# The first weights by one-partition rows and eighths, and the router's products beside the first maxima, in an attention and expert kernel

## The chip, the cores and the metric

The kernel runs on one core of a Trainium2 chip. The metric is device time in microseconds (us) of one execution; lower is better. TensorE multiplies matrices, VectorE (DVE), ScalarE (ACT) and GpSimd (POOL) work on vectors, and SyncE (SP) issues most of the transfers between memory and the core. Every engine works through its own list of instructions in order and waits where an instruction needs another engine or a transfer.

## The reference

Four sequences of 512 tokens with 256 numbers each go through two residual blocks. In the first, each sequence has its own expert, chosen by the largest of eight numbers in `cond_8`; its three matrices make a gated layer, and 16 heads of attention with one shared key and value follow. In the second, the weights of a linear layer are mixed from eight matrices by the same numbers, and a router sends each token to two of eight experts with a capacity of 128 rows per group.

```python
expert = jnp.argmax(opcode_onehot, axis=-1)
hidden = jax.nn.silu(up) * gate           # up, gate: x with the expert's two matrices
out = jnp.einsum('bsh,bdh->bsd', hidden, wd) + bd[:, None, :]
...
w_bot = jnp.einsum('bg,got->bot', y, weight * mask[None, :, :])
x2 = jnp.einsum('bnt,bot->bno', x, w_bot) + bias
...
logits = jnp.einsum('gth,he->gte', xg, w_router)
...
x = x + attn(cond(x, cond_8))
x = x + ffn(cond2(x, cond_8))
```

All of it is in float32.

## The kernel before

The program is one long list written out by hand; the order in the text is the order on each engine. It has four stages.

**The start.** SP loads `cond_8`, broadcast to 128 partitions (`cond_sb`, L86), and the transposed x of sequence 0. VectorE works out `rows` (L114 to L122): for each sequence the row at which its expert's weights begin, with the partition's own number added (`rowp`), so that an indirect transfer can use it too. SP reads the row of partition 0 into a register (L159) and `load_cond` issues the weights of the sequence: the up and gate matrices in quarters (`w`, 256 KB each, L162) and, behind the first quarter, the down matrix with the three biases (`wd`, 517 KB, L164). Sequences 0, 1 and 2 are loaded so; those of sequence 3 by two indirect transfers of POOL (`fetch_cond`, L147). Until weights are there TensorE multiplies a tile of zeros, seven times (L94). [...]

**The gated layer.** `hidden(b, hc)` (L280) computes one of four blocks of 128 hidden units: two products for up into the only bank of tag "a" (L291), two for gate into a bank of tag "x" (L293), Silu on ScalarE with its bias from `wd` (L295), the product on VectorE (L296). `down(b, dc)` (L275) follows. VectorE mixes the weights of the second block in between (`mixed`, L262 and L264, into `wb_sb`), four operations at a time.

**Attention.** A unit of work is a step; a sequence has 16, the kernel 64. Step n has two parts on TensorE: `maxima` of the step six ahead (four products in 32-row tiles, L387, each read by one VectorE reduction, L391) and `exponentials` of its own (four such products, L416, each read by one ScalarE operation, L420). `weigh` (L434, 32-column tiles) multiplies the exponentials of the step before with the values. Before step 0 lies the lead: six `maxima`, each with a piece of the gated layer of sequence 3 or 2 behind it (`before_steps`, L808). `beside` (L734) lists what else is put into each of a sequence's steps: entries (1, ...) work for the next sequence (queries, keys, values `v`), (-1, ...) and (-2, ...) for those before (output projection, `rT`, `mix`, router, scatter of rows). `behind` (L772) adds four calls to sequence 0: at steps 5 and 9 `turn_mixed` (L700: four transposes of `wb_sb`, a copy by ScalarE) of two sequences, at steps 7 and 11 `route_mixed` (L711: the product of these with the router's matrix, so that the router's logits come out of the same product as the layer itself; for sequence 0 also that of the bias).

A step whose side work has TensorE products is `dense`: its order is maxima, exponentials, side work, maxima, exponentials, both halves of `weigh`. Any other step puts half of `weigh` between the two halves. The names that make a step dense are in `ON_PE` (L770).

**The experts.** The rows are gathered in tiles of up to 256, with two products and a weighted scatter-add each. The change doesn't touch this stage.

PSUM has eight banks: three of tag "m", one "a", four "x" (`BANKS`, L72).

Of the kernel before, what the change touches and what calls it, by code (L numbers as in the profile page):

```python
# [10 lines left out]
F32 = mybir.dt.float32  # L11
I32 = mybir.dt.int32
AF = mybir.ActivationFunctionType
ALU = mybir.AluOpType
AX = mybir.AxisListType
PSUM = bass.MemoryType.PSUM

P = 128
B = 4
# [3 lines left out]
NE = 8  # L23
# [14 lines left out]
WROW = 1024 + 10  # L38
# [3 lines left out]
def adaln_attn_ffn_kernel(  # L42
# [22 lines left out]
    nc = tc.nc  # L65
    mm = nc.tensor.matmul

    const = ctx.enter_context(tc.tile_pool(name="const", bufs=1))
# [6 lines left out]
    def bank(tag):  # L75
# [6 lines left out]

    od = tc.dram_tile([B, 4, P, T], F32, name="od")

    cond_sb = const.tile([P, B, NE], F32, name="cond_sb")
    nc.sync.dma_start(  # L86
        cond_sb.rearrange("p b e -> p (b e)"), cond[0:1, :].to_broadcast([P, B * NE])
    )


    nil = const.tile([P, 512], F32, name="nil")
    nc.vector.memset(nil, 0.0)
    for _ in range(7):
        mm(bank("x"), nil[:, 0:P], nil, start=True, stop=True)  # L94
    nc.scalar.activation(const.tile([P, 1], F32, name="nil1"), nil[:, 0:1], AF.Silu)

# [1 line left out]
    rev = const.tile([P, NE], F32, name="rev")  # L98
    nc.gpsimd.iota(
        rev, pattern=[[-1, NE]], base=NE, channel_multiplier=0,  # L100
        allow_small_or_imprecise_dtypes=True,
    )

    rowp = const.tile([P, 1], F32, name="rowp")
    nc.gpsimd.iota(
        rowp, pattern=[[0, 1]], base=NE * P, channel_multiplier=1,
        allow_small_or_imprecise_dtypes=True,
    )


    rows = const.tile([P, B], I32, name="rows")
    top = const.tile([P, B], F32, name="top")
    first = const.tile([P, B, NE], F32, name="first")
    nc.vector.tensor_reduce(top, cond_sb, AX.X, ALU.max)  # L114
    nc.vector.tensor_tensor(
        first, cond_sb, top.unsqueeze(2).to_broadcast([P, B, NE]), ALU.is_equal
    )
    nc.vector.tensor_tensor(
        first, first, rev.unsqueeze(1).to_broadcast([P, B, NE]), ALU.mult
    )  # L120
    nc.vector.tensor_reduce(top, first, AX.X, ALU.max)
    nc.vector.tensor_scalar(rows, top, -float(P), rowp, ALU.mult, ALU.add)  # L122

    attn_ctx = ctx.enter_context(ExitStack())
    apool = attn_ctx.enter_context(tc.tile_pool(name="apool", bufs=1))
# [11 lines left out]
    def cond_tiles():  # L137
        w = wexp.tile([P, 2, F], F32, name="wi_sb").rearrange("p c f -> p (c f)")
        w2 = wexp.tile([P, F // P, D], F32, name="wo2_sb").rearrange("p c f -> p (c f)")
        w_of.append((w, w2))  # L140
        return w, w2

    def fetch_cond(b):

        w, w2 = cond_tiles()
        for t, src in ((w, wcond), (w2[:, 0:WROW], wcond2)):
            nc.gpsimd.indirect_dma_start(  # L147
                out=t,
                out_offset=None,
                in_=src,  # L150
                in_offset=bass.IndirectOffsetOnAxis(ap=rows[:, b : b + 1], axis=0),
            )

    def load_x(b):
        nc.sync.dma_start(xT_sb[:, :, ts(b, T)], xT[:, :, ts(b, T)])

    def load_cond(b):

        row = nc.sync.value_load(rows[0:1, b : b + 1], min_val=0, max_val=(NE - 1) * P)  # L159
        w, wd = cond_tiles()  # L160
        for hc in range(4):
            nc.sync.dma_start(w[:, ts(hc, 512)], wcond[ds(row, P), ts(hc, 512)])  # L162
            if hc == 0:
                nc.sync.dma_start(wd[:, 0:WROW], wcond2[ds(row, P), :])  # L164


    load_x(0)
    load_cond(0)
    load_x(1)
    load_cond(1)  # L170
    nc.sync.dma_start(m2_sb, mask2.rearrange("p c o -> p (c o)"))
# [6 lines left out]
    def load(ap, shape, name):  # L178
# [22 lines left out]
        out=upto, in_=ones, compare_op=ALU.is_ge, fill=0.0, base=0,  # L201
        pattern=[[1, P]], channel_multiplier=-1,
    )
    def numbers(name, shape, pattern, base, step):
# [20 lines left out]
        out=through, in_=ones[:, 0 : NE * NE].rearrange("p (a e) -> p a e", a=NE),  # L225
        compare_op=ALU.is_ge, fill=0.0, base=0, pattern=[[1, NE], [-1, NE]],
        channel_multiplier=0,
# [35 lines left out]
        else:  # L263
            nc.vector.scalar_tensor_tensor(wb, w, c, wb, ALU.mult, ALU.add)  # L264

    fetch_cond(3)
    mixing = [(b, g) for b in range(B) for g in range(NE)]
    hid_of = {}

# [441 lines left out]
    def route_mixed(b):  # L711
# [23 lines left out]
        [(1, "q0"), (-2, "rank0")],  # L735
        [(1, "q1"), (-2, "rank1")],
        [(-1, "values"), (1, "k"), (-2, "places"), (-2, "rows")],
        [(1, "v"), (-2, "send")],
        [(-1, "inv"), (-2, "row0")],
        [(-2, "row1")],  # L740
        [(-1, "norm0"), (-1, "norm1"), (-2, "row2")],
        [(-1, "out0"), (-1, "out1"), (-2, "row3")],
        [(-1, "out2"), (-1, "out3")],
        [(-1, "rT0"), (-1, "rT1")],
        [(-1, "mix0"), (-1, "mix1")],
        [(-1, "mix2"), (-1, "mix3")],
        [],
# [21 lines left out]
    ]  # L769
    ON_PE = ("q", "k", "v", "out", "rT", "mix")  # L770

    behind = {  # L772
        5 + 2 * b + 2 * n: (f, b) for b in range(0, B, 2)
        for n, f in enumerate((turn_mixed, route_mixed))
    }

    final = {
        0: ["inv0"], 2: ["values1"], 4: ["inv1", "norm0", "norm1"],
        6: ["out0", "out1", "out2", "out3"], 7: ["rT0", "rT1"],
# [7 lines left out]
    def side(b, k):  # L787

        for off, name in (last if b == B - 1 else beside)[k]:
            to = b + off  # L790
            if not 0 <= to < B:
                continue
            if name[:5] == "pairs":
                first_pairs(name[5:])
                continue
            if off == 1:
                if name == "q0":
                    projection[to] = project(to)
                projection[to][name]()
            else:  # L800
                work[to][name]()
        if b == 0 and k in behind:
            f, to = behind[k]
            f(to)
            f(to + 1)


    before_steps = [  # L808
        [(hidden, B - 1, 0), (down, B - 2, 0)],
        [(down, B - 2, 1), (hidden, B - 1, 1)],  # L810
        [(hidden, B - 1, 2)],
        [(hidden, B - 1, 3)],
        [(down, B - 1, 0)],
        [(down, B - 1, 1)],
    ]
    for m in range(LEAD):
        maxima(m, (0, 1, 2, 3))
        if m == 3:
            shifted(0)
        for f, b, k in before_steps[m]:  # L820
            f(b, k)
        while mixing:
            mixed(*mixing.pop(0))
    c1.close()
# [237 lines left out]
    for n in range(STEPS + 1):  # L1062
        m = n + LEAD
        if n in (0, 26, 42, 56):
            residual((0, 26, 42, 56).index(n))
        b, k = divmod(n, 16)
        names = [name for _, name in (last if b == B - 1 else beside)[k]] if b < B else []
        dense = (b == 0 and k in behind) or any(
            name.rstrip("0123") in ON_PE and (b > 0 or name in projection[0]) for name in names
        )  # L1070
        if m >= STEPS:
            if n < STEPS:
                exponentials(n, (0, 1, 2, 3))
            if n == STEPS:

                up(0, 0)
            weigh(n - 1, (2, 3))
            weigh(n - 1, (0, 1))
            if n < STEPS:
                side(b, k)  # L1080
        elif dense:

            maxima(m, (0, 1))
            exponentials(n, (2, 3))
            side(b, k)
            maxima(m, (2, 3))
            exponentials(n, (0, 1))
            if n > 0:
                weigh(n - 1, (2, 3))
                weigh(n - 1, (0, 1))  # L1090
        else:

            maxima(m, (0, 1))
            exponentials(n, (2, 3))
            if n > 0:
                weigh(n - 1, (2, 3))
            maxima(m, (2, 3))
            exponentials(n, (0, 1))
            side(b, k)
            if n > 0:  # L1100
                weigh(n - 1, (0, 1))
        if m < STEPS and m % 4 == 3:
            shifted(m // 4)
# [153 lines left out]
```

## Time and profile before

| | us |
|---|---|
| median of three runs (lowest, highest) | 665.79 (663.47, 666.86) |
| the profiled execution's own time | 666.94 |
| its span | 665.1 |
| TensorE busy | 645.8 (97%) |
| VectorE busy | 323.8 (49%) |
| ScalarE busy | 225.8 (34%) |
| POOL busy | 112.8 (17%) |
| start to first real product | 10.09 |
| lead (six maxima) | 70.8 to 105.9 |
| 64 steps begin | 105.85 |

The span is the time between the first and the last instruction in one profiled execution; its own time has the launch around it. In the profile a float32 product counts as two passes, so "x4" of L291 are two products. A busy TensorE is one whose passes follow each other, whatever they compute. The share of the clock granted was 0.99: half speed from about 371 to 375 us, at the start until about 6, and full elsewhere.

### The profile page before, as it was taken

The page shows a single profiled execution, that of the slowest core. Times are in us where ns is not written, and L with a number is a line of the kernel's source. Part 1 is how long each engine was busy: PE and PEld are TensorE (multiplying, and loading weights), DVE is VectorE, ACT ScalarE, POOL GpSimd, SP SyncE. Part 2 cuts the span into 40 slices and gives each one's busy share as a digit, 9 for nine tenths or more (in the row PEclk, how much of TensorE's full clock was granted, in tenths as well). Part 3 has the DMA queues.
Part 4 walks back from the last instruction along what each step waited for, and adds up shares of the span by engine and source line. Part 5 has one row for each costly group of instructions (what it writes and reads, how often), then busy time and mean ns, then how long its engine had stood idle before and what let it go on. Part 6 is the DMA issues. An engine that isn't in the chain of part 4 may idle for free.

```text
span 665.1 us, 10593 instructions
## 1 busy us (share of the span) xinstructions
PE 645.8 (97%) x3994; PEld 394.3 (59%) x3994; DVE 323.8 (49%) x782; ACT 225.8 (34%) x400; POOL 112.8 (17%) x149
## 2 busy tenths in 40 slices
PE   9999999999999999999999899999999999999991
PEld 3444433444334434343344378888999999988881
DVE  1164854666667677867976625372222222221210
ACT  1122114665664565546545541322011111121110
POOL 1600000000000000400040412235321222222231
PEclk9999999999999999999999899999999999999996
DMA  6942982200132114320134399329799999974411
GB/s 217 384 137 65 300 270 81 62 17 17 43 106 94 35 31 133 132 65 18 50 132 138 107 389 283 111 97 310 230 288 314 326 333 316 353 232 115 89 19 24
DMA packets 65147, 107.47 MB, mean 162 GB/s; under 512 B 6848, under 2 KB 26944, under 8 KB 64960
## 3 DMA queue, kind: packets, MB, share of 16 engines
q1 hardware_dynamic: 49200, 86.38, 38.8%
q0 software_dynamic: 7008, 10.63, 7.9%
q10 hardware_dynamic: 8880, 9.71, 4.6%
q8 instruction: 33, 0.54, 0.3%
q14 instruction: 26, 0.21, 0.1%
HBM read 79.59 MB, written 26.98 MB: 160 GB/s over the span
## 4 chain that ended last, share of the span: by engine, by line
PE 95%; DVE 1%; DMA 1%; issue 1%; POOL 0%; SPq 0%; POOLq 0%; DVEq 0%
PE ps_m L387 20%; PE ps_m L996 19%; PE ps_x L1026 18%; PE ps_a L434 10%; PE ps_a L291 4%; PE ps_x L275 4%; PE ps_x L293 4%; PE ps_x L514 2%; PE ps_x L546 2%; PE ps_x L325 2%; PE ps_x L416 2%; PE ps_x L94 1%; PE ps_x L340 1%; PE ps_a L981 1%; PE ps_x L535 1%
## 5 line engine op out<-in xcount | busy, mean ns | idle before, releaser
L391 DVE TENSOR_REDUCE negm<-ps_m 128x1 f32<-128x512 f32 x250 | 160.6, 685 | 64.8 <-PE ps_x L416 52.1
L420 ACT ACTIVATE e<-ps_x 128x512 f32<-128x512 f32 x244 | 132.5, 594 | 112.9 <-PE ps_x L416 100.3
L387 PE MATMUL ps_m<-k,q 32*128 32x512 f32 x500 | 151.7, 639 | 0.4 <-DVE negm L391 0.4
L416 PE MATMUL ps_x<-q,k 32*128 32x512 f32 x488 | 141.5, 643 | 1.4 <-DMA q<-nmT 1.4
L996 PE MATMUL ps_m<-xT,wi_sb 128*128 128x128 f32 (+1 forms) x800 | 130.3, 321 | 0.0
L1026 PE MATMUL ps_x<-wo_sb,e 128*128 128x256 f32 x576 | 128.5, 379 | 0.0
L996 PEld LDWEIGHTS ps_m<-xT,wi_sb 128*128 128x128 f32 x800 | 118.9, 191 | 10.1 <-issue 0.4
L1026 PEld LDWEIGHTS ps_x<-wo_sb,e 128*128 128x128 f32 x576 | 107.6, 190 | 13.8 <-issue 0.2
L1000 ACT ACTIVATE e<-ps_m 128x512 f32<-128x512 f32 x72 | 42.8, 597 | 193.8 <-PE ps_m L996 158.3
L387 PEld LDWEIGHTS ps_m<-k,q 32*128 32x128 f32 x500 | 45.7, 183 | 56.6 <-issue 24.4
L1037 POOL DMA_INDIRECT out_dram<-y,to_row x36 | 56.0, 1557 | 127.9 <-DVE y L1036 36.2
L434 PE MATMUL ps_a<-e,v 128*32 128x256 f32 x1024 | 75.6, 391 | 0.5 <-issue 0.3
L434 PEld LDWEIGHTS ps_a<-e,v 128*32 128x32 f32 x1024 | 24.0, 109 | 77.7 <-issue 64.3
L983 DVE COPY xT<-ps_a 128x256 f32<-128x256 f32 (+1 forms) x23 | 12.2, 529 | 99.5 <-PE ps_a L981 94.0
L1036 DVE TENSOR_SCALAR y<-ps_x,w 128x256 f32<-128x256 f32 x36 | 17.4, 483 | 77.2 <-PE ps_x L1026 77.2
L667 POOL DMA_INDIRECT xp<-x,to_i x32 | 32.0, 1000 | 57.7 <-DVE negm L391 28.5
L416 PEld LDWEIGHTS ps_x<-q,k 32*128 32x128 f32 x488 | 39.1, 183 | 4.5 <-issue 4.3
L596 POOL TENSOR_SCALAR x<-mk 128x4 f32<-128x4 f32 x4 | 0.8, 209 | 209.3 <-DVE mk L593 209.3
L296 DVE SCALAR_TENSOR_TENSOR hid<-ps_x,wo_sb,sg 128x512 f32<-128x512 f32 x16 | 12.0, 749 | 46.2 <-PE ps_x L293 46.2
L291 PE MATMUL ps_a<-xT_sb,wi_sb 128*128 128x512 f32 x64 | 30.5, 598 | 0.0
L293 PE MATMUL ps_x<-xT_sb,wi_sb 128*128 128x512 f32 x64 | 30.1, 592 | 0.0
L1034 POOL CAST to_row<-at 128x1 int32<-128x1 f32 x36 | 19.0, 527 | 58.5 <-DVE at L1019 58.5
(153 smaller groups left out, 444.1 us busy)
## 6 DMA issues: line engine op xcount, KB each, us to landing
wi_sb<-in_wi_dram SPq DMA_DIRECT2D x25, 1024.0 KB
wo_sb<-in_wo_dram SPq DMA_DIRECT2D x25, 1024.0 KB
xp<-zeros ACTq DMA_DIRECT2D x1, 8712.0 KB
q<-qd SPq DMA_DIRECT2D x8, 512.0 KB
od<-stage SPq DMA_DIRECT2D x15, 256.0 KB
wi_sb<-in_wcond_dram SPq DMA_DIRECT2D x12, 256.0 KB
xt<-xp SPq DMA_DIRECT2D x11, 264.0 KB
xT_sb<-in_xT_dram SPq DMA_DIRECT2D x4, 512.0 KB
```

The source lines that it names most:

```text
L291: mm(pu, wu[:, c, :], xT_sb[:, c, ts(b, T)], start=c == 0, stop=c == 1)
L293: mm(pg, wg[:, c, :], xT_sb[:, c, ts(b, T)], start=c == 0, stop=c == 1)
L387: mm(pm, q[32 * j : 32 * j + 32, i, ts(hg, P)], k[32 * j : 32 * j + 32, :], start=True, stop=True,)
L391: nc.vector.tensor_reduce(nm[:, i, j : j + 1], pm, AX.X, ALU.max, negate=True)
L416: mm(px, k[rows_j, ts(sc, P)], seqs[u // 4]["q"][rows_j, :, ts(u % 4, P)], start=True, stop=True,)
L420: nc.scalar.activation(e_of[n][:, :, j, :].rearrange("p h (i t) -> p i h t", i=4), px.rearrange("p (i h t) -> p i h t", i=4, h=4), AF.Exp,)
L434: i = mm(pa_of[u][32 * hh : 32 * hh + 32, j0 * P : (j0 + nj) * P], seqs[b]["v"][:, sc, :], e[:, hh, j0 : j0 + nj].rearrange("p j n -> p (j ...
L667: i = nc.gpsimd.indirect_dma_start(out=xp, out_offset=bass.IndirectOffsetOnAxis(ap=s["to_i"][:, k, ch : ch + 1], axis=0), in_=s["x3"][:, c ...
L996: mm(ph[:, ts(k, n)], wi_of[u][:, c, ts(f0 + k, P)], xT_of[u][:, c, :], start=c == 0, stop=c == 1,)
L1000: nc.scalar.activation(hT_of[u][:, f0 : f0 + each].rearrange("p f t -> p (f t)"), ph, AF.Gelu_apprx_tanh,)
L1026: mm(po[:, 0:D], hT_of[u][:, fc, ts(h, P)], wo_of[u][:, fc, :], start=fc == 0, stop=fc == F // P - 1,)
L1037: i = nc.gpsimd.indirect_dma_start(out=out_rows, out_offset=bass.IndirectOffsetOnAxis(ap=to, axis=0), in_=y, in_offset=None, compute_op=AL ...
```

## The change

`cond_8` is loaded to one partition (`cond1`) and the rows are worked out there, without the partition's number; the broadcast `cond_sb`, which `mixed` needs, is loaded behind the first sequence's weights. Sequence 0's first quarter of up and gate becomes two transfers of 256 columns, the first for up, the second for gate. Sequence 3's weights are loaded by `load_cond` like the others. Four products on zeros are left of seven. `turn_mixed` and `route_mixed` move from steps 5 to 11 of sequence 0 into the lead, and the next sequence's values `v` from step 3 to step 9.

```diff
-    cond_sb = const.tile([P, B, NE], F32, name="cond_sb")
-    nc.sync.dma_start(
-        cond_sb.rearrange("p b e -> p (b e)"), cond[0:1, :].to_broadcast([P, B * NE])
-    )
+    cond1 = const.tile([1, B, NE], F32, name="cond1")
+    nc.sync.dma_start(cond1.rearrange("p b e -> p (b e)"), cond)
...
-    for _ in range(7):
+    for _ in range(4):
         mm(bank("x"), nil[:, 0:P], nil, start=True, stop=True)
...
-    nc.vector.tensor_scalar(rows, top, -float(P), rowp, ALU.mult, ALU.add)
+    nc.vector.tensor_scalar(rows, top, -float(P), float(NE * P), ALU.mult, ALU.add)
...
-        for hc in range(4):
-            nc.sync.dma_start(w[:, ts(hc, 512)], wcond[ds(row, P), ts(hc, 512)])
-            if hc == 0:
+        parts = [ts(0, 256), ts(1, 256)] if b == 0 else [ts(0, 512)]
+        for n, part in enumerate(parts + [ts(hc, 512) for hc in range(1, 4)]):
+            nc.sync.dma_start(w[:, part], wcond[ds(row, P), part])
+            if n == len(parts) - 1:
                 nc.sync.dma_start(wd[:, 0:WROW], wcond2[ds(row, P), :])
...
     load_x(0)
     load_cond(0)
+    cond_sb = const.tile([P, B, NE], F32, name="cond_sb")
+    nc.sync.dma_start(
+        cond_sb.rearrange("p b e -> p (b e)"), cond[0:1, :].to_broadcast([P, B * NE])
+    )
     load_x(1)
...
-    fetch_cond(3)
+    load_cond(3)
...
-        [(1, "v"), (-2, "send")],
+        [(-2, "send")],
...
-        [(-1, "rT0"), (-1, "rT1")],
+        [(-1, "rT0"), (-1, "rT1"), (1, "v")],
...
-    behind = {
-        5 + 2 * b + 2 * n: (f, b) for b in range(0, B, 2)
-        for n, f in enumerate((turn_mixed, route_mixed))
-    }
...
-        if b == 0 and k in behind:
-            f, to = behind[k]
-            f(to)
-            f(to + 1)
...
         [(hidden, B - 1, 0), (down, B - 2, 0)],
-        [(down, B - 2, 1), (hidden, B - 1, 1)],
-        [(hidden, B - 1, 2)],
-        [(hidden, B - 1, 3)],
-        [(down, B - 1, 0)],
+        [(down, B - 2, 1), (hidden, B - 1, 1), (turn_mixed, 0), (turn_mixed, 1)],
+        [(hidden, B - 1, 2), (route_mixed, 0), (route_mixed, 1), (turn_mixed, 2)],
+        [(hidden, B - 1, 3), (route_mixed, 2), (turn_mixed, 3)],
+        [(down, B - 1, 0), (route_mixed, 3)],
         [(down, B - 1, 1)],
```

The one-partition forms of L115 and L118, the loss of `rowp` and `fetch_cond`, and the shorter test for `dense` follow from these.

## The prediction

> **What bounds the kernel now.** I read the page first, then the chain of waits, then the timeline of the first 15 us, then TensorE's timeline through the stretches that the change touches. The page's chain gives one owner:
>
> ```profile
> PE 95%; DVE 1%; DMA 1%; issue 1%; POOL 0%; SPq 0%; POOLq 0%; DVEq 0%
> ```
>
> The reader is to see that only time taken off TensorE counts, or time in which it works on nothing useful. There is such a time at the start. The chain of waits in order of time (start, us, what):
>
> ```profile
> 1.53 8.56 PE ps_x L94 x14
> 10.09 1.95 PE ps_a L291 x4
> 12.04 1.72 PE ps_x L293 x4
> 13.76 1.72 PE ps_a L291 x4
> ```
>
> L94 are the seven products on zeros, in two passes each: TensorE is "busy" from 1.53 but does nothing of the result until 10.09. From there the chain holds TensorE's instructions without a break to 105.85. What the first real product waits for stands in the timeline (start, us, engine, line):
>
> ```profile
> 0.81 0.40 SPq L86 DMA_DIRECT2D cond_sb<-in_cond_dram  x1
> ...
> 3.90 0.19 DVE L114 TENSOR_REDUCE top<-cond_sb 128x4 f32<-128x32 f32 x1 [2.43 <-DMA cond_sb<-in_cond_dram]
> ...
> 4.95 0.23 DVE L122 TENSOR_SCALAR rows<-top,rowp 128x4 int32<-128x4 f32 x1
> ...
> 6.23 0.38 SPq L162 DMA_DIRECT2D wi_sb<-in_wcond_dram  x1
> ...
> 6.80 0.33 SPq L164 DMA_DIRECT2D wo_sb<-in_wcond_dram  x1
> ...
> 12.16 0.69 ACT L295 ACTIVATE sg<-ps_a,wo_sb 128x512 f32<-128x512 f32 x1 [9.85 <-DMA wo_sb<-in_wcond_dram]
> ```
>
> Here the chain is cond, five VectorE operations, the register load on SP (5.18 to 6.23), the first weights. The last line matters most: the first Silu needs its bias, which comes with the second weight transfer (L164), and ran only at 12.16. It holds the one bank of tag "a", so the next block's L291 cannot start before it ends.
>
> The other end of the change is in the steps of sequence 0. TensorE's timeline, maxima that open steps 4 to 8 and what steps 5 and 7 hold:
>
> ```profile
> 124.81 0.70 PE L387 MATMUL ps_m<-k,q 32*128 32x512 f32 x2
> ...
> 128.35 0.70 PE L387 MATMUL ps_m<-k,q 32*128 32x512 f32 x2
> ...
> 129.43 1.09 PE L705 MATMUL ps_x<-ident,wb_sb 128*128 128x128 f32 x8
> 130.45 0.70 PE L387 MATMUL ps_m<-k,q 32*128 32x512 f32 x2
> ...
> 132.79 0.70 PE L387 MATMUL ps_m<-k,q 32*128 32x512 f32 x2
> ...
> 136.32 0.70 PE L387 MATMUL ps_m<-k,q 32*128 32x512 f32 x2
> ...
> 137.40 1.06 PE L717 MATMUL ps_x<-wr_sb,stage 128*128 128x8 f32 x8
> 138.31 0.59 PE L723 MATMUL ps_x<-wr_sb,bias2p_sb 128*128 128x8 f32 x4
> 138.76 1.04 PE L717 MATMUL ps_x<-wr_sb,stage 128*128 128x8 f32 x8
> ...
> 141.79 0.70 PE L387 MATMUL ps_m<-k,q 32*128 32x512 f32 x2
> ```
>
> A plain step lasts 3.54 us (124.81 to 128.35; 132.79 to 136.32 is 3.53). Step 5 with two turns lasts 4.44, step 7 with two routes and the bias 5.47. Last, the table by stretches shows the lead (the six maxima ahead of step 0), where the router's products go, as full (columns: length, PE, PEld, DVE, ACT, POOL, clock, DMA share, GB/s):
>
> ```profile
> 70.80:105.90 35.10, 35.10 (x117) 13.56 (x116) 24.11 (x39) 4.81 (x7) 0.11 (x1) 1.00 0.83 264
> ```
>
> TensorE has no gap there, so nothing placed there is free; VectorE and ScalarE have 11 and 30 us to spare.
>
> [...] passes of L94 follow each other by 0.86 us until 5.96 and by 0.43 after 6.50; and after 370 to 372, where TensorE worked 0.74 of 2 us, its clock reads 0.50 in 372 to 374. [...] four transposes take 0.44 between full-array products (L981) and 0.58 between row-tiled ones (L347, 121.92 to 122.50).
>
> **The change part by part.**
>
> *Four products on zeros.* Three fewer are six passes of 0.43 at the full clock: 2.58. TensorE is free at 10.09 - 2.58 = 7.51. The clock had risen by 6.50, so four suffice here.
>
> *Cond on one partition.* Its landing is not shown. The broadcast was done on its first engine at 2.55 and on its last at 3.88 (landing marks of the trace). Bounds: no gain, or 1.6 us; I take 1.4, so VectorE starts at 2.5. The five operations keep their length (0.19 each with 128 partitions or with one; bound: 0.2 less in all). The first weights are issued at 6.23 - 1.4 = 4.83.
>
> *First weights by eighths.* One more issue, 0.57 (6.23 to 6.80). The first eighth is half of the 256 KB that had landed by 9.95 at the latest; with the issue 1.4 earlier and half the bytes I put it at 7 to 8.5, near the 7.51. But the bias transfer is now third: 4.83 + 2 x 0.57 = 5.97 against 6.80, so 0.83 earlier. Silu starts at 12.16 - 0.83 = 11.33, ends at 12.02, and the second block's L291 starts at 12.05. It started at 13.59 in the timeline. Gain 1.5, not the 2.6 of the products removed: this wait is late next. If the transfers move by the full 1.4, gain 2.1; if cond gains nothing, Silu is at 12.7, gain 0.2.
>
> *The broadcast cond_sb, now an issue of its own behind the first weights (SP), and sequence 3's weights by SP instead of POOL.* Each extra SP issue delays what is behind it by about 0.5; the next queued is x of sequence 1, landed by 15.4 and first needed at 23.89 (the fifth L291 group). cond_sb is first used by L262 at 38.56. The five issues of sequence 3 stand in front of the query stores L331, for which SP waited 35.8 us in all on ScalarE (SP's own waits, first 120 us); that covers some 3.5 us. POOL loses 2.1 us of issue that nobody waited for. Weights are wanted at 71.91. Cost nothing; without the cover, up to 3.5 us.
>
> *Router's products from steps 5, 7, 9, 11 into the lead.* Removed: step 5, 4.44 - 3.54 = 0.90; step 7, 1.93; step 9 (4.44, and then 3.97 because v comes there) 0.47; step 11 (153.30 to 158.33, 5.03) 1.49; step 3, which loses v, 3.97 - 3.54 = 0.43. Sum 5.22. The gain per step is less than the products' own length, since a plain step waits some 0.26 in its second half for VectorE to free a bank, which the products had filled. Added in the lead, next to full-array products[...]: 4 x 0.44 for turns, 4 x 0.87 for routes[...], 0.45 for the bias: 5.69. Net +0.5. Five small copies of 0.17 go to VectorE and four of 0.6 to ScalarE, into their spare time.
>
> *v from step 3 to step 9, sequences 1 and 2.* Step 3 gives 0.43 in sequence 1. In sequence 2 it lasts 4.69 with the send work of VectorE, which stays (a plain step with such work took 3.74 in sequence 3, and the next one 3.70): 0.75 or less. Step 9 already has eight transposes (215.04); four more are 0.44, and the second exponential then waits for the first copy of rT: +0.48 each. Net -0.25 (between -0.7 and +1.0).
>
> **Sum.** -1.5 + 0.5 - 0.25 = -1.25 us. Against the profiled execution's 666.94 (span 665.1) that is 665.7. It lies 1.15 over the median of the three runs, 665.79; the same difference on the median gives 664.5.
>
> **The rivals.**
>
> *The full start, and the clock.* The bias lands early enough, gain 2.6, and the halved clock at 372, which costs 1.7 (3.4 us at half), falls away [...]. [...] Against: nothing in the change moves that stall. 665.79 - 2.6 + 0.25 - 1.7 = 661.7. Chance 0.17.
>
> *No net effect.* The landings stay where bandwidth sets them (332 to 407 GB/s from 11 to 16 us), the start yields 0.2, the lead costs 0.5, step 9 as much again: 666.4. For it: Silu's wait on its bias. Against: the transfers are waiting for their issue, not for bandwidth, until 9 us. Chance 0.2.
>
> *Slower: the clock falls at the start.* The zeros end at 7.5; [...] The start gain is then gone (first product at 10.9 against 10.09: +0.8), [...] with +0.25 from the rest some 669. For it: 370 to 374 shows that this happens. Against: 256 KB with a later issue had landed by 9.95. Chance 0.06[...].
>
> That the lead stalls on banks of tag "x" is the same sign but small: VectorE has 3.8 us of work in a lead step that lasts 5.5 or more.
>
> **How the numbers follow.** Forecast 664.5 with chance 0.57 (own range 663.0 to 666.0). The runs before already spread by 3.4 us, and 0.5% (3.3 us) is about what a measurement of this kernel can tell from no change. Faster by over 0.5% needs under 662.5: the first rival and a tail of the forecast, 0.18. Slower by over 0.5%: over 669.1, part of the last rival and what I don't see, 0.06. Within: 0.76. The range that leaves out 2 in 10 is 661.8 to 667.0.
>
> **What would show it.** Right: L94 with 8 passes; the first weights issued at about 4.8; L291's first at 7.5 to 8.5; a gap of TensorE ahead of its second block, ended by Silu L295 at about 11.3, that block at about 12; the lead 5.7 longer; steps 3, 5, 7, 11 of sequence 0 at 3.54 and step 9 at 3.97; step 9 of sequences 1 and 2 near 4.95. Wrong: a lead longer by over 7 us, plain steps over 3.6, passes of 0.86 after 8 us, or a second block that starts before 11.2 or after 13.

## The result, and the profile after

The changed kernel takes 663.49 us (median of 22 runs, 662.41 to 665.11), beside 664.73 us for the kernel before on the same chip (22 runs, 663.24 to 667.07): a ratio of 0.9974, with an interval of 0.9965 to 0.9984. A second comparison, 663.68 against 665.33 us, gives the same ratio, 0.9974 (0.9962 to 0.9986). The profiled execution has a span of 661.6 us (665.1 before).

Lines of the changed file have other numbers: L92 are the products on zeros (L94 before), L278 and L280 the up and gate products (L291, L293), L282 the Silu (L295), L262 the down products (L275), L374 the maxima (L387), L403 the second scores (L416), L692 a turn (L705), L704 and L710 a route and its bias (L717, L723), L334 the transposes for v (L347), L522 those for rT (L535).

The page's chain after, by engine:

```profile
PE 88%; DMA 6%; DVE 3%; issue 1%; SPq 1%; POOL 0%; POOLq 0%; DVEq 0%
```

TensorE owned 95% before. Little of that shift is the start: of DMA's 6%, some 40 us, it holds 5.9 us. Over half lies in three stretches far behind it (268.48 to 274.22, 381.12 to 392.86 and 392.90 to 402.22). Another profile of the same kernel has PE at 89% and DMA at 4%, so these shares are not laid to the change. What the start waits for stands in the chain of waits, in order of time (start, us, what):

```profile
0.82 1.21 DMA cond<-in_cond_dram
...
6.05 4.68 DMA wi_sb<-in_wcond_dram
...
10.87 1.95 PE ps_a L278 x4
```

The products on zeros have left the chain. In their place stand the small load of cond and a transfer of weights that ends as the second block (the next 128 hidden units) starts. The timeline of the same stretch (start, us, engine, line, operation; in brackets the idle time before it and what ended it):

```profile
1.54 5.39 PE L92 MATMUL ps_x<-nil 128*128 128x512 f32 x8 [1.54 <-DVE nil L90]
2.06 0.17 DVE L106 TENSOR_REDUCE top<-cond 1x4 f32<-1x32 f32 x1 [0.57 <-DMA cond<-in_cond_dram]
...
4.40 0.95 SPq L145 DMA_DIRECT2D wi_sb<-in_wcond_dram  x2
...
5.53 0.33 SPq L147 DMA_DIRECT2D wo_sb<-in_wcond_dram  x1
...
9.68 0.69 ACT L282 ACTIVATE sg<-ps_a,wo_sb 128x512 f32<-128x512 f32 x1 [7.36 <-DMA wo_sb<-in_wcond_dram]
...
10.87 0.67 PE L278 MATMUL ps_a<-xT_sb,wi_sb 128*128 128x512 f32 x1 [0.26 <-DMA wi_sb<-in_wcond_dram]
```

The first real product starts at 6.94 (10.09 before), the second block at 10.87 (13.59 before). Silu still waits for its bias, but only until 9.68, and is done at 10.37; what ends last ahead of the second block is no longer Silu but the second quarter of the weights, at 10.73. In the second profile of this kernel it is Silu again, by little: it ends at 10.47 and the block starts at 10.62. TensorE alone needs 3.51 us from the first block to the second (10.09 to 13.59 before is 3.50), so without any wait the block would start at 10.45.

The router's products stand in the lead as written. TensorE's timeline, what the second and third lead step hold beside their maxima:

```profile
84.30 1.04 PE L692 MATMUL ps_x<-ident,wb_sb 128*128 128x128 f32 x8
...
89.88 0.95 PE L704 MATMUL ps_x<-wr_sb,stage 128*128 128x8 f32 x8
90.69 0.59 PE L710 MATMUL ps_x<-wr_sb,bias2p_sb 128*128 128x8 f32 x4
91.13 1.04 PE L704 MATMUL ps_x<-wr_sb,stage 128*128 128x8 f32 x8
92.03 0.64 PE L692 MATMUL ps_x<-ident,wb_sb 128*128 128x128 f32 x4
```

They run without a gap, one behind the other: 89.88 to 92.59 is 2.71 us for one step's share. In the steps of sequence 0 the reader reads the starts of the maxima, the first of each step:

```profile
127.30 0.70 PE L374 MATMUL ps_m<-k,q 32*128 32x512 f32 x2
...
130.84 0.91 PE L374 MATMUL ps_m<-k,q 32*128 32x512 f32 x2
...
134.38 0.90 PE L374 MATMUL ps_m<-k,q 32*128 32x512 f32 x2
...
137.91 0.91 PE L374 MATMUL ps_m<-k,q 32*128 32x512 f32 x2
...
141.45 0.90 PE L374 MATMUL ps_m<-k,q 32*128 32x512 f32 x2
```

Four steps of 3.54 us each, steps 5 and 7 among them, which had lasted 4.44 and 5.47.

Such starts, read from TensorE's timeline of every run, divide the span. This table, in us, is what the rest argues from (the lead is the six maxima ahead of step 0; the last column is where sequence 3's first step starts, so it holds all that the change touches):

| kernel | first product | second block | length of the lead | sequence 0 | sequence 1 | sequence 2 | start of sequence 3 |
|---|---|---|---|---|---|---|---|
| before | 10.09 | 13.59 | 35.08 | 67.18 | 70.38 | 71.69 | 315.10 |
| after | 6.94 | 10.87 | 40.65 | 62.41 | 70.51 | 72.20 | 313.89 |
| difference | -3.15 | -2.72 | +5.57 | -4.77 | +0.13 | +0.51 | -1.21 |

From the second block to the lead the two differ by 0.07 more, so the start is worth 2.65 at the lead's first step (70.77 to 68.12). The sum, -2.65 + 5.57 - 4.77 + 0.64, is the -1.21 of the last column. The two profiled spans differ by 3.5; the rest arises behind that column, 0.98 of it in step 6 of sequence 3, 8.64 us before and 7.66 after. That step read 7.65 to 8.32 in the experiments, whichever part of the change they held, so that share is not laid to the change. -1.21 us lies inside the interval of the ratio (-1.1 to -2.3 us on 664.73).

### The profile page after: what moved, and what is told of

It reads as the page before. It is cut to its first block, busy times and chain, and to the rows that moved or that the text cites. A ratio compares the mean times of both kernels' runs of the same rounds, so it can differ in the third digit from the quotient of the medians.

```text
span 661.6 us, 10602 instructions
## 1 busy us (share of the span) xinstructions
PE 642.0 (97%) x3988; PEld 393.3 (59%) x3988; DVE 324.2 (49%) x782; ACT 226.0 (34%) x400; POOL 111.6 (17%) x146
## 4 chain that ended last, share of the span: by engine, by line
PE 88%; DMA 6%; DVE 3%; issue 1%; SPq 1%; POOL 0%; POOLq 0%; DVEq 0%
PE ps_m L374 19%; PE ps_x L1005 17%; PE ps_m L975 16%; PE ps_a L421 10%; PE ps_x L262 4%; PE ps_a L278 4%; PE ps_x L280 4%; PE ps_x L533 2%; PE ps_x L312 2%; PE ps_x L403 2%; PE ps_x L501 2%; DMA wo_sb<-in_wo_dram 2%; DMA inv<-od 1%; PE ps_x L327 1%; PE ps_a L960 1%
## 5 line engine op out<-in xcount | busy, mean ns | idle before, releaser
L374 PE MATMUL ps_m<-k,q 32*128 32x512 f32 x500 | 152.3, 639 | 0.4 <-DVE negm L378 0.4
L403 PE MATMUL ps_x<-q,k 32*128 32x512 f32 x488 | 139.6, 642 | 1.9 <-DMA q<-nmT 1.9
L374 PEld LDWEIGHTS ps_m<-k,q 32*128 32x128 f32 x500 | 46.5, 183 | 55.7 <-DVE negm L378 25.4
L421 PE MATMUL ps_a<-e,v 128*32 128x256 f32 x1024 | 76.6, 392 | 0.1
L421 PEld LDWEIGHTS ps_a<-e,v 128*32 128x32 f32 x1024 | 23.3, 109 | 80.2 <-issue 66.5
L403 PEld LDWEIGHTS ps_x<-q,k 32*128 32x128 f32 x488 | 38.2, 184 | 4.4 <-issue 4.2
L278 PE MATMUL ps_a<-xT_sb,wi_sb 128*128 128x512 f32 x64 | 30.5, 599 | 0.3 <-DMA wi_sb<-in_wcond_dram 0.3
L280 PE MATMUL ps_x<-xT_sb,wi_sb 128*128 128x512 f32 x64 | 30.1, 592 | 0.0
```

The costliest lines, as they stand in the source:

```text
L278: mm(pu, wu[:, c, :], xT_sb[:, c, ts(b, T)], start=c == 0, stop=c == 1)
L280: mm(pg, wg[:, c, :], xT_sb[:, c, ts(b, T)], start=c == 0, stop=c == 1)
L374: mm(pm, q[32 * j : 32 * j + 32, i, ts(hg, P)], k[32 * j : 32 * j + 32, :], start=True, stop=True,)
L403: mm(px, k[rows_j, ts(sc, P)], seqs[u // 4]["q"][rows_j, :, ts(u % 4, P)], start=True, stop=True,)
L421: i = mm(pa_of[u][32 * hh : 32 * hh + 32, j0 * P : (j0 + nj) * P], seqs[b]["v"][:, sc, :], e[:, hh, j0 : j0 + nj].rearrange("p j n -> p (j ...
```

## Experiments: each part alone

Theory A, once the two traces lay side by side: the start brings the whole gain, more than forecast, and the two moves behind it each cost something, so that most of it is given back. Its rival B stands, with its own numbers, in the expectations.

**The start alone.** From the changed kernel, the lead's lists, `behind`, its test and the place of v are put back:

```diff
-        [(down, B - 2, 1), (hidden, B - 1, 1), (turn_mixed, 0), (turn_mixed, 1)],
+        [(down, B - 2, 1), (hidden, B - 1, 1)],
...
+        if b == 0 and k in behind:
...
-        [(-1, "rT0"), (-1, "rT1"), (1, "v")],
+        [(-1, "rT0"), (-1, "rT1")],
```

> The start of the change alone (cond on one partition, eighths, four products on zeros, sequence 3's weights by SP); router's products and v stay where they were before. Theory A (the start gives all of the gain, the router's products and v together give back about 1): the lead begins near 68.1 us as in the changed kernel, the steps are those of before, time about 2.6 us below before (ratio 0.996) and about 1 below the changed kernel. Theory B (the router's move pays, the start gives only the forecast 1.5): about 1.5 below before, ratio 0.998, and above the changed kernel.

**The router's products alone,** the same lists moved in the kernel before:

```diff
-        [(down, B - 2, 1), (hidden, B - 1, 1)],
+        [(down, B - 2, 1), (hidden, B - 1, 1), (turn_mixed, 0), (turn_mixed, 1)],
...
-        if b == 0 and k in behind:
```

> The router's products in the lead alone, everything else as before (v at step 3). Theory A: the lead 5.6 us longer, steps 5, 7, 9, 11 of sequence 0 at about 3.54 each and together some 5.2 less 0.4 shorter, so 0.3 to 0.9 us slower than before (ratio 1.0005 to 1.0015). Theory B (it relieves VectorE and ScalarE and so the later stall at step 6 of sequence 3): 0.5 to 1.5 faster than before, step 6 of sequence 3 at 7.7 against 8.6.

**v alone,** moved from step 3 to step 9 in the kernel before:

```diff
-        [(1, "v"), (-2, "send")],
+        [(-2, "send")],
...
-        [(-1, "rT0"), (-1, "rT1")],
+        [(-1, "rT0"), (-1, "rT1"), (1, "v")],
```

> v from step 3 to step 9 alone. Theory A: step 3 0.4 to 0.6 shorter, step 9 of sequences 1 and 2 0.48 longer, step 4 of sequence 2 0.6 longer: 0 to 0.7 us slower than before in all. Theory B (v's move is the gain, a dense step becomes a plain one): 0.5 to 1 faster.

Measured, with each kernel's ratio to the kernel before on the same chip. That kernel took 668.25 us in this comparison, 3.5 more than beside the change, so that ratios can be set beside the change's 0.9974 and medians cannot:

| kernel | median us, runs | ratio, interval | second block | lead | sequence 0 | sequence 1 | sequence 2 |
|---|---|---|---|---|---|---|---|
| the start alone | 664.28, 7 | 0.9941, 0.9926 to 0.9956 | 10.86 | 35.08 | 70.45 | 70.36 | 71.71 |
| the router's products alone | 669.02, 22 | 1.0013, 1.0002 to 1.0024 | 13.65 | 40.65 | 62.38 | 70.37 | 71.87 |
| v alone | 668.99, 22 | 1.0010, 0.9997 to 1.0023 | 13.61 | 35.08 | 67.16 | 70.51 | 71.95 |

The start alone is faster than the whole change. The router's products alone add 5.57 to the lead and take 4.80 from sequence 0: +0.77, which its ratio shows too (+0.9 us on 668.25). v alone adds 0.13 in sequence 1 and 0.26 in sequence 2; its ratio (+0.7 us, from -0.2 to +1.5) agrees with that and includes 1. Theory A holds and B falls. Two readings need care. The start alone was 2.9 to 4.9 us faster by its ratio, and its steps show 2.65: a few tenths of a us have no place in its trace, and seven runs are few. And its sequence 0 lasted 70.45 in the profiled execution against 67.18, although it has that part from the kernel before; the section on narrow products follows that up.

## Experiments: the parts of the start

Each puts one part back and leaves the rest as changed. In turn: seven products on zeros, the first quarter of the weights in one transfer, cond loaded as a broadcast to 128 partitions (the arithmetic still on one), and, the other way, only two products on zeros:

```diff
-    for _ in range(4):
+    for _ in range(7):
```

> The changed kernel with seven products on zeros instead of four. Theory A (the products bind the start as soon as the weights come earlier): first real product at 9.5 to 10.1, second block at about 13.6, the whole start gain gone: about 2.6 us above the changed kernel, 0.8 to 1.4 above before. Theory C (transfers bind the start, the products are only filling): the second block stays near 10.9 to 12, within 1 us of the changed kernel.

```diff
-        parts = [ts(0, 256), ts(1, 256)] if b == 0 else [ts(0, 512)]
+        parts = [ts(0, 512)]
```

> The changed kernel with sequence 0's first quarter in one transfer of 256 KB again. If the eighth lets TensorE begin early: first real product 0.5 to 1.2 us later than 6.94, but the bias and second quarter are issued 0.5 earlier, so the second block starts at 10.4 to 11.4 and the time is within 0.5 us of the changed kernel. If the eighths carry the gain: 1 us or more slower than the changed kernel.

```diff
-    cond1 = const.tile([1, B, NE], F32, name="cond1")
-    nc.sync.dma_start(cond1.rearrange("p b e -> p (b e)"), cond)
+    cond1 = const.tile([P, B, NE], F32, name="cond1")
+    nc.sync.dma_start(cond1.rearrange("p b e -> p (b e)"), cond[0:1, :].to_broadcast([P, B * NE]))
```

> The changed kernel with cond loaded broadcast to 128 partitions again, the rows still worked out on one. If the landing of the broadcast is what one partition saves: VectorE begins at 3.9 instead of 2.06, first weights issued at 6.2, TensorE idle from 6.9 to about 8.6, second block at about 12.7, 1.8 us above the changed kernel. If the operations on one partition save it: VectorE begins near 2.1 and nothing changes.

```diff
-    for _ in range(4):
+    for _ in range(2):
```

> The changed kernel with two products on zeros. The products end near 5.0, the first eighth lands at 6.8. If the clock's rise needs the zeros up to the weights: the first real passes are 0.86 us apart until the clock rises, second block 1 to 3 us later than 10.87, time 0.5 to 2.5 above the changed kernel. If the time since the first product counts alone: first product at 6.8 to 6.9 at full clock, no change within 0.3 us.

The kernel before took 668.62 us in the comparison of the last three, 668.25 in that of the first:

| kernel | median us, runs | ratio, interval | first product | second block | later than the change's 10.87 by |
|---|---|---|---|---|---|
| seven on zeros | 669.84, 20 | 1.0016, 1.0001 to 1.0030 | 9.57 | 13.00 | 2.13 |
| first quarter whole | 666.90, 18 | 0.9979, 0.9965 to 0.9994 | 8.39 | 11.90 | 1.03 |
| cond as a broadcast | 667.19, 20 | 0.9988, 0.9978 to 0.9998 | 8.55 | 12.47 | 1.60 |
| two on zeros | 666.40, 20 | 0.9969, 0.9957 to 0.9980 | 6.97 | 12.51 | 1.64 |

The three losses, 2.13, 1.03 and 1.60, add up to 4.76, well over the 2.72 that the three parts bring together. The load of cond, the issue and the transfer lie in a row, the products on zeros run beside them, and TensorE starts when the later of the two is done. These are losses at the second block, each in one profile; three profiles of the changed start have it at 10.87, 10.86 and 10.62. The ratios, set beside the change's, give 2.8, 0.3 and 0.9 us, each known to about 1.2 us: the time alone shows a loss for seven products, and not for the whole quarter.

None of the parts was tried alone in the kernel before. One profile bears on it: the kernel with three times the routes (below) starts as before, and its products on zeros ended at 9.38, yet TensorE then waited 0.81 us for the weights:

```profile
10.19 1.96 PE L291 MATMUL ps_a<-xT_sb,wi_sb 128*128 128x512 f32 x4 [0.81 <-DMA wi_sb<-in_wcond_dram]
```

In the profile before, zeros and weights ended within 0.14 us of each other (10.09 and 9.95), so that fewer products on zeros alone should gain next to nothing there; this was not run. With seven products on zeros the second block came at 13.00, not at the 13.6 expected. TensorE itself is late and no wait for a transfer is left, as the timeline shows:

```profile
9.57 1.88 PE L278 MATMUL ps_a<-xT_sb,wi_sb 128*128 128x512 f32 x4
...
11.49 0.69 ACT L282 ACTIVATE sg<-ps_a,wo_sb 128x512 f32<-128x512 f32 x1 [9.17 <-PE ps_a L278]
...
13.00 1.88 PE L278 MATMUL ps_a<-xT_sb,wi_sb 128*128 128x512 f32 x4
```

With cond as a broadcast the load is what it was before, and all behind it is late. The same view of that kernel:

```profile
3.89 0.17 DVE L106 TENSOR_REDUCE top<-cond 1x4 f32<-1x32 f32 x1 [2.41 <-DMA cond<-in_cond_dram]
...
7.13 0.33 SPq L147 DMA_DIRECT2D wo_sb<-in_wcond_dram  x1
...
11.36 0.69 ACT L282 ACTIVATE sg<-ps_a,wo_sb 128x512 f32<-128x512 f32 x1 [9.04 <-DMA wo_sb<-in_wcond_dram]
```

Against 2.06 that is 1.83 on the load. The five VectorE operations behind it take 1.28 us before (3.90 to 5.18), 1.28 after (2.06 to 3.34), and 1.08 here on one partition (3.89 to 4.97): what one partition is worth lies in the transfer. After the change the load to one partition is a single packet of data (128 bytes), with landing marks at 1.30 and 2.04 us in the trace; the broadcast before has sixteen, between 2.55 and 3.88. The first was in use by VectorE 1.24 us after its issue (0.82 to 2.06), the broadcast after 3.07 (0.82 to 3.89).

The eighths do more than let the first product start on less. By the trace's landing marks a transfer of a whole quarter had its first mark at 8.28 and its last at 9.95 before, and at 6.51 and 8.25 with the quarter whole; the marks of the eighths lie within 0.57 and 0.55 (6.23 to 6.80, 6.79 to 7.34). And the transfer with the biases, behind them, took 4.06 us from its issue after the change and 4.14 with cond as a broadcast, but 4.90 with the quarter whole and 5.27 before. Issued 0.54 earlier than with eighths, it then landed 0.30 later (9.89 against 9.59). All profiles agree on the direction: behind eighths the bias transfer took 4.06 to 4.21 us in six of them, behind a whole quarter 4.42 to 5.27 in six, of which the profile before has the longest. So the split is the cause, and it is worth some 0.6 us on this transfer; why the last marks of a 256 KB transfer lag is not shown.

The second block of that kernel, 11.90, missed what was expected of it: the first product came at 8.39 as expected, but from there TensorE needs its 3.51 us whatever has landed.

Two products on zeros let the first block run at half the clock in the profiled execution (TensorE's timeline):

```profile
1.54 3.78 PE L92 MATMUL ps_x<-nil 128*128 128x512 f32 x4 [1.54 <-DVE nil L90]
6.97 3.75 PE L278 MATMUL ps_a<-xT_sb,wi_sb 128*128 128x512 f32 x4 [1.65 <-DMA wi_sb<-in_wcond_dram]
10.52 2.16 PE L280 MATMUL ps_x<-xT_sb,wi_sb 128*128 128x512 f32 x4
12.51 1.88 PE L278 MATMUL ps_a<-xT_sb,wi_sb 128*128 128x512 f32 x4
```

The first group lasts 3.75 instead of 1.95, and the clock rose at 11.1 (5.0 after the change). Yet over 20 runs this kernel's ratio, 0.9969, is no worse than the change's 0.9974. In the other thirteen profiles, with at least four products on zeros, the clock rose anywhere between 4.72 and 6.55. Whether it rose earlier than 11.1 in other executions of this kernel, one profiled execution doesn't show, and why its median is no worse stays open.

## Experiments: a start without waits

If the waits are what is left at the start, the biases should go ahead of the other quarters and the down weights, first needed much later, behind them. The start alone, with this order for sequence 0:

```diff
...
-                nc.sync.dma_start(wd[:, 0:WROW], wcond2[ds(row, P), :])
...
+        nc.sync.dma_start(w[:, ts(1, 256)], wcond[ds(row, P), ts(1, 256)])
+        nc.sync.dma_start(wd[:, 1024:WROW], wcond2[ds(row, P), 1024:WROW])
+        for hc in range(1, 4):
+            nc.sync.dma_start(w[:, ts(hc, 512)], wcond[ds(row, P), ts(hc, 512)])
+        nc.sync.dma_start(wd[:, 0:1024], wcond2[ds(row, P), 0:1024])
```

> The start of the change alone (as in the run of the start alone), and sequence 0's ten columns of biases as a transfer of their own behind the two eighths, with the down matrix behind the up and gate matrices. Theory A (the second block waits for its quarter of weights, which shares the engines with the 517 KB in front of it): the wait of 0.26 us in front of the second block goes, the second block starts at about 10.5, time 0.2 to 0.4 below the run of the start alone, so about 2.9 below before. Against it: the biases are 40 bytes a row and may land late, Silu then holds the bank: second block at 11 or later and no gain.

It took 664.18 us (6 runs), ratio 0.9944 (0.9925 to 0.9963), and its second block started at 10.59. Beside the 0.9941 of the start alone no gain in time is shown. It was run again in the second comparison, beside the change itself:

> The changed kernel itself, beside the next run on the same chip. Ratio to before 0.996 to 0.9985 again; lead near 68.1, 40.6 long; step 0 of sequence 3 some 1.2 us earlier than in the kernel before.

> The start alone with the biases as a transfer of their own, once more beside the changed kernel. If leaving the router's products and v in their steps is better by what the parts say (0.8 and 0.6 us, and 0.3 for the biases): about 1.7 us below the changed kernel, ratio to before 0.994 to 0.9965. Sequence 2, which lasted 73.04 us in the one profile so far, at 71.7 as elsewhere if that was chance.

There the change took 663.68 (22 runs), and this kernel 661.74 (9 runs, 660.98 to 663.92), ratio to the kernel before 0.9949 (0.9932 to 0.9966): it beats both. Sequence 2 lasted 71.59, so the 73.04 was chance. The timeline of its start (L285 and L289 are L278 and L282 of the change):

```profile
6.97 1.95 PE L285 MATMUL ps_a<-xT_sb,wi_sb 128*128 128x512 f32 x4
...
8.96 0.69 ACT L289 ACTIVATE sg<-ps_a,wo_sb 128x512 f32<-128x512 f32 x1 [6.64 <-PE ps_a L285]
...
10.48 1.88 PE L285 MATMUL ps_a<-xT_sb,wi_sb 128*128 128x512 f32 x4
```

Silu is now released by the product it works on, not by its bias, and the second block follows the first after 3.51 us, TensorE's own time. Its sequence 3 starts at 311.87, against 313.80 in the change's profile beside it: 1.93 us, and the medians differ by 1.94. Of that, 0.22 lies ahead of the lead, 0.14 at the second block (10.62 in that profile of the change); the rest is that it leaves the router's products and v where they were.

## Experiments: narrow products and the clock

In the profile of the start alone the clock is at half from 138.3 and again from 155.4, 3.4 us each. TensorE's timeline there, the first of the two (L421 is `weigh`):

```profile
134.73 1.06 PE L704 MATMUL ps_x<-wr_sb,stage 128*128 128x8 f32 x8
135.65 0.59 PE L710 MATMUL ps_x<-wr_sb,bias2p_sb 128*128 128x8 f32 x4
136.09 1.04 PE L704 MATMUL ps_x<-wr_sb,stage 128*128 128x8 f32 x8
...
138.13 1.78 PE L421 MATMUL ps_a<-e,v 128*32 128x256 f32 x16
```

No gap of TensorE lies ahead of it, only the products with 8 columns and, from 137.06, the step's own row-tiled ones. Sequence 0 is 3.27 us longer for the two, and the profiled execution took 667.53 us where the six others took 664.04 to 664.62. Theory K: products that narrow count for the clock as little work. In the kernel before, the routes are made three times over (the same sums, written again), and in another the turns instead, which have 128 columns:

```diff
-        for c in range(2):
+        for c in (0, 1) * 3:
             for oc in range(2):
                 mm(
                     pt[:, ts(c, NE)], wbT[:, oc, c, :], wr_sb[:, oc, :],
```

> The kernel before with each route's four eight-column products done three times over (the same results). In the profile of the start alone the clock fell to half for 3.4 us right behind the routes of steps 7 and 11; in the kernel before it did not. Theory K [...] two drops between 135 and 175 us, steps 7 and 11 longer by 3.5 each plus 1.7 for each drop. Theory N (the drops are chance, products keep the clock whatever their width): no drop there, steps 7 and 11 at about 9.0 and 8.5.

```diff
-        for oc in range(2):
+        for oc in (0, 1) * 3:
             for c in range(2):
                 nc.tensor.transpose(
```

> The kernel before with each turn's four transposes done three times over (the same results), 24 in steps 5 and 9, some 2.7 us. Beside the run with the routes: if it is the eight columns that count as idle, transposes of 128 columns keep the clock, no drop between 125 and 175 us, steps 5 and 9 at about 5.9. If transposes count as idle too, a drop behind step 5 or 9.

With three times the routes, the one run took 681.67 us, and sequence 0 83.86 instead of 67.18. Its table by stretches (length, PE, PEld, DVE, ACT and POOL busy, clock, DMA share, GB/s) around steps 7 and 11, where the routes run from 137.50 and from 162.79:

```profile
130.00:135.00 5.00, 5.00 (x50) 2.32 (x52) 3.45 (x7) 3.71 (x8) 0.00 (x0) 1.00 0.15 56
...
142.00:152.00 10.00, 10.00 (x57) 5.21 (x58) 2.17 (x5) 1.65 (x4) 0.00 (x0) 0.53 0.01 2
152.00:165.00 13.00, 13.00 (x116) 6.46 (x116) 8.62 (x14) 8.48 (x17) 0.00 (x0) 1.00 0.06 22
165.00:176.00 11.00, 11.00 (x62) 7.61 (x61) 1.64 (x4) 1.09 (x2) 0.00 (x0) 0.53 0.00 0
```

TensorE is busy throughout, and the clock is at half for 10.2 us from within each of the two groups (from 141.25 and from 165.15), three times as long as Theory K had allowed. With three times the turns (668.26 us, one run) one drop came, of 3.4 us, and not behind the turns. TensorE's timeline:

```profile
129.37 2.84 PE L705 MATMUL ps_x<-ident,wb_sb 128*128 128x128 f32 x24
...
138.82 1.06 PE L717 MATMUL ps_x<-wr_sb,stage 128*128 128x8 f32 x8
139.73 0.59 PE L723 MATMUL ps_x<-wr_sb,bias2p_sb 128*128 128x8 f32 x4
140.18 1.04 PE L717 MATMUL ps_x<-wr_sb,stage 128*128 128x8 f32 x8
...
141.73 1.07 PE L387 MATMUL ps_m<-k,q 32*128 32x512 f32 x2
```

24 transposes in a row left the clock as it was (1.00 from 130 to 138); the drop, at 141.6, follows the eight products of two routes and their bias, which this kernel leaves as they were. K expected no drop here, and missed that the single routes are enough; that they are is what the start alone had shown.

Which group brings a drop is not settled by the time spent on narrow products. In four profiles the changes of the clock were found multiples of 3.413 us apart. Before, it is full from 6.17 to 371.39, at half for 3.413 and full again for 279.89, which is 107, 1 and 82 times 3.413; after the change it is the same from 4.98 on. The two falls of the start alone lie 17.1 us apart (5 times), those with three times the routes 23.9 (7 times). Cut into stretches of that length from the first rise on, two profiles have the two routes of step 11, 1.88 us, within one stretch: in the start alone (153.36 to 155.24) the clock fell at its end, in the kernel before (154.38 to 156.26) it did not.

Columns come closer, without settling it. A pass of 512 columns takes 0.43 us at the full clock, 0.84 ns a column; a pass of 8 columns takes 0.12 us, but at that price it counts for 0.007. Now count each pass in a stretch by its columns, passes side by side once. This is an estimate from the passes in the traces, since some records are missing. In the profile before, the stretch ahead of the fall at 371.39, where TensorE waits for other things, holds 1.35 us. Of the 187 others at the full clock up to TensorE's last product, the two with the routes of steps 7 and 11 hold 1.37 each, and all the rest 2.38 or more; none has a fall at its end. After the change the stretch ahead of the fall at 370.21 holds 1.09, and the 186 others 1.50 or more, the lowest of them the one with routes in the lead.

The stretches ahead of the falls behind narrow products hold 1.24 and 1.38 in the start alone, 0.21 and 1.03 with three times the routes, 1.03 with three times the turns. So both kinds of drop follow stretches with little so counted; but 1.37 without a fall and 1.38 with one show that this count alone doesn't tell them apart. In the lead of the router's products alone the routes and their bias ran for 2.15 us (92.58 to 94.73) between full-array products, and the clock stayed full (1.00 from 88 to 98.1).

## Why the prediction was right, and which terms were off

The forecast of 664.5 us stands 1.0 over the measured 663.49, since the kernel before itself read 664.73 in 22 runs where three had given 665.79. Its sum, -1.25, stands beside -1.24 between the medians and the -1.21 of the steps. That it fits so well is luck: its three terms were off by -1.15, +0.30 and +0.89 us, which cancel. One of its own signs of being wrong came true as well: the second block started before 11.2.

- *The start, -1.5 forecast, -2.65 measured.* Half of the mechanism was right: the products on zeros are no longer the bound, and a transfer is late next. The other half was not: the forecast had the second block wait for the bias by about 1 us, and in this profile it waits 0.26 us for the second quarter of the weights (start at 10.87, where TensorE alone would give 10.45). The term that failed is "the bias transfer is now third ... 0.83 earlier". Cond gave 1.84, not 1.4, so that the issue moved by 1.27 (6.80 to 5.53). And the sum let the transfer take as long as in the profile before; it took 1.21 less (5.27 to 4.06). About half of that is the split of the quarter in front of it, and the rest is that 5.27 was the longest of five profiles with that start (4.42 to 5.27): the forecast took one execution's landing for the kernel's. Silu so came at 9.68, not at 11.33. The first product, at 6.94, is 0.57 earlier than forecast, because the clock rose at 4.98 instead of 6.17, which is chance. The full start of the first rival, 2.6, did come; that rival fell by its other half, the drop near 372, which is there at 370.2 as before. In four other profiles it is absent, those of the router's products alone, v alone, the whole quarter and three times the turns: whether it comes changes from one execution to the next.
- *The router's products, +0.5 forecast, +0.80 measured.* The lead's +5.69 came as +5.57. Steps 3, 5, 7 and 11 became plain steps of 3.54, as forecast. The rest was lost in steps whose length was taken as given: step 9 lasts 4.17, not 3.97, step 8 3.69 instead of 3.54, and step 15 4.18 instead of 4.09.
- *v in sequences 1 and 2, -0.25 forecast, +0.64 measured (+0.39 with v alone), within its bounds of -0.7 to +1.0 but of the other sign.* Step 9 came at 4.97 in both, +0.48 as forecast, and step 3 of sequence 1 at 3.54. Two items went wrong. Step 3 of sequence 2 gave 0.63, but step 4 took back 0.62 (4.16 instead of 3.54). VectorE's list for these steps (start, us), two lines of before and then four of after, shows why:

```profile
261.65 0.28 DVE L649 TENSOR_TENSOR at<-hot,row 128x32 f32<-128x32 f32 x2
...
262.72 1.28 DVE L391 TENSOR_REDUCE negm<-ps_m 128x1 f32<-128x512 f32 x2
```

```profile
260.83 1.29 DVE L378 TENSOR_REDUCE negm<-ps_m 128x1 f32<-128x512 f32 x2 [0.94 <-PE ps_x L403]
262.04 0.28 DVE L636 TENSOR_TENSOR at<-hot,row 128x32 f32<-128x32 f32 x2
...
263.02 0.17 DVE L648 TENSOR_TENSOR to_i<-pos,to 128x8 int32<-128x8 f32 x1
263.10 1.28 DVE L378 TENSOR_REDUCE negm<-ps_m 128x1 f32<-128x512 f32 x2
```

  The send work, 262.04 to 263.10, stands now between the maxima of step 4, which start at 261.31; before, it stood at 261.65 to 262.72, inside step 3, which ran from 258.96 to 263.66. The same VectorE work holds the same banks, one step later. The forecast named this ("and the next one 3.70") and then took the gain in full. Step 7, which the forecast did not count, lasts 6.19 in sequence 1 and 6.34 in sequence 2 instead of 6.09 and 6.02, and step 6 of sequence 2 gave 0.27. v alone shows the 6.19 and the 0.27. The 6.34 is not v's doing: in five other profiles with v at step 3 that step lasted 6.20 to 7.68.
- *What was put at nothing,* SP's and POOL's issues and the copies, stayed at nothing: no step of sequence 0 beyond those named is longer, and the way from the second block to the lead by 0.07 only.
- *The other rivals.* "No net effect" (whose items add up to 666.6, not 666.4) fell with the start. Half the clock in the first block came only with two products on zeros, and there in the profile, not in the median.

## What to carry to other kernels

Where a small load, an issue and a transfer wait on each other in a row, with products on zeros beside them, put the parts back one at a time: here each was worth 1.0 to 2.1 us at the second block with the others in place, and all together 2.7. Where two paths end within 0.2 us of each other, as the zeros and the first weights did before, shortening one of them frees next to nothing. Read a landing from more than one profile before a sum rests on it. Look for the small operand that rides in a large transfer (here the biases): sent ahead, it took away the last wait, though too little for the times to show. A transfer cut in two in front of another can let both land earlier (here the first product came at 6.94 instead of 8.39, and the biases landed at 9.59 instead of 9.89). Work moved out of a step only pays if the step does not hand its VectorE work to the next one, and if the place it goes to has a gap.

## What the runs showed of the hardware that was not expected

TensorE's clock fell to half while TensorE's passes followed each other without a gap, behind products with 8 columns: for 3.4 us with single routes, for 10.2 us with three times as many; 24 transposes of 128 columns in a row (129.37 to 132.14) did not bring it down. In the kernel before, two stretches of 3.413 us that held, counted by columns, an estimated 1.37 us of products brought no fall; in the start alone one with 1.38 did. The two drops in one execution cost 3.27 us, more than the whole change is worth.

The first load of 256 KB had its last landing mark 1.5 to 1.75 us behind its first in six profiles (1.67 before), and two loads of half the size within 0.5 to 0.65 us each, in eight (0.57 and 0.55 after the change).
